# Reordering the attention stage of a two-layer graph network: key scores per feature block, two products earlier, adjacency banks later, degrees through DRAM

## The chip, the cores and the metric

The kernel runs on one core of a Trainium2 chip. The metric is the device time of one execution in microseconds (us). Three runs of the kernel before gave a median of 375.6 us. One more execution was taken with the hardware profiler; all rows quoted below are from that one.

Engines are named as in the profile: PE is TensorE's matmul side and PEld its weight loads, DVE is VectorE, ACT is ScalarE, POOL is GpSimd, SP is SyncE, which here only issues DMAs. Times inside the kernel are counted from the start of the profiled span.

## The reference, cut to what matters

The graph has N = 1250 nodes with 512 features and E = 20000 edges sorted by destination. Two layers follow each other, each behind a layer norm and a ReLU. The change touches the first one:

```python
h  = relu(layernorm(x))
xn = batchnorm(h)                                  # over the nodes
agg = segment_sum(xn[src], dst) / max(deg, 1)      # deg: edges per destination
conv = relu(agg @ W_conv + b_conv)
# attention over the first 256 nodes, 8 heads of 64, 256 random features (proj)
q, k, v = heads(h[:256] @ Wq), heads(h[:256] @ Wk), heads(h[:256] @ Wv)
phi(t) = exp(t*s @ proj.T - 0.5*sum((t*s)**2) - max) / sqrt(256) + 1e-6
kv  = phi(k).T @ v
att = (phi(q) @ kv) / (phi(q) @ phi(k).sum() + 1e-6) @ Wo
x = x + batchnorm(conv + att + h)
```

For keys the max runs over all nodes of a head, for queries over one row. The second layer (a sum over neighbours and two dense layers) is not touched.

## The kernel before, in words

**Opening (`tile_gnn`).** The edge lists are read as overlapping pieces, and for each group of 10 destinations the 256 edges that hold its own are picked by matmuls with 0/1 matrices (L1568, tile `keys`: 20 passes for the sources, 20 for the destinations). DVE then splits the keys into `js`, `prow`, `kcol` (L1606 to L1608) and ACT copies `dist` (L1609). TensorE is kept busy meanwhile by matmuls on zeros (`keep_up`, L1517: six ahead of the counting `cnt`, three ahead of `keys`). A branch on `bad` follows; the arm taken is `sorted_graph`.

**Attention stage (`sorted_graph`, L137 to L527).** Four kinds of work share the engines:

- *The adjacency matrix*, 25 banks of 50 destinations. `onehots` (L198) makes two 0/1 tiles on DVE (`op` and `ok`, L206), `count` (L213) multiplies them in ten matmuls on PE, and ACT copies the bank to `adj` (L220). The one-hot tiles have two buffers, the banks two PSUM buffers (`acc`), which `product` shares.
- *Nodes.* `layernorm_relu` (L86) takes statistics on DVE (L96), scales on ACT (L105), PE transposes (L226) and ACT copies to `hT` (L227). Nodes 0 and 1 come from the opening, eight tiles of nodes follow.
- *Keys and queries.* `features` (L236) multiplies four blocks of weights with `hT` (L245, eight passes each), scales and squares them on ACT (L249, L251), and sums the squares per head in `pd` by a matmul with the 128 x 8 tile `half` (L248, L253). `scores` (L263) multiplies with the projection into the one PSUM tile `sc`. For keys ACT copies it to `kf` (L333) and DVE takes the maximum `kmx` (L334); `kf` gets its exponentials later (L376). Values are L337.
- *`product(j)`* (L416): batch norm of tile j of the nodes (`normed`), four matmuls with `W_conv` (L422, eight passes), and the result split into `hi` and `lo`.

`beside()` is a generator that yields after each piece of this; the loop at L404 takes one bank between two of its pieces, 15 banks in all. In it, all four key blocks come first, then the eight key scores with the values, then the queries. After it the loop at L493 runs ten turns: `query(i)`, `product(i)`, in turn 1 all of `keyvalue` (L449), in turns 2 to 7 `degrees` (L428: one-hot tile, two matmuls, maximum and reciprocal on 128 x 210 elements), one bank, `turn(i-1)` (L472) and `attend(i-2)` (L482). The output projection (L521) ends the stage, and the sum over neighbours (L575) follows from 135 us on.

Each engine runs its instructions in a fixed order, which a scheduler sets when the kernel is built; `order(...)` around an instruction keeps those so marked in the order of the program.

Of the kernel before, what the change touches and what calls it, by code (L numbers as in the profile page):

```python
# [23 lines left out]
KD = D // 128  # L24
# [45 lines left out]
def sorted_graph(ctx: ExitStack, tc: tile.TileContext, ed, x, n1g, n1b, n2g, n2b, wconv, bconv,  # L70
# [99 lines left out]
    load_x(x1, (NT, NT + 1), (NT + 1, NT + 3), (NT + 3, NJ - 1))  # L170
# [17 lines left out]
    half = ap1.tile([128, KD, HEADS], F32, name="half")  # L188
    nc.gpsimd.memset(half, 0.0)
    for b in range(KD):  # L190
        for a in range(2):
            nc.gpsimd.memset(half[a * 64:a * 64 + 64, b, 2 * b + a:2 * b + a + 1], 0.5)
# [20 lines left out]
    def count(bt, op, ok):  # L213
        acc = accp.tile([S, NJ, TB], F32, name="acc", tag="acc")
        for q in range(BG):
            for i in range(2):
                nc.tensor.matmul(acc[:, :, q * TG:(q + 1) * TG], op[:, q, :, i],  # L217
                                 ok[:, q, :, i].rearrange("p (j t) -> p j t", t=TG),
                                 start=(q == 0 and i == 0), stop=(q == BG - 1 and i == 1), skip_group_check=True)
        nc.scalar.copy(adj[:, :, bt * TB:(bt + 1) * TB], acc)  # L220
# [15 lines left out]
    def features(wt, name):  # L236

        tT = ap1.tile([128, KD, TOK], F32, name=f"{name}T", tag="tT")
        dg = ap1.tile([128, NT, HEADS], F32, name=f"{name}_dg")

        pd = mm.tile([HEADS, TOK], F32, name="mm")
        for b in range(KD):
            ps = mm.tile([128, TOK], F32, name="mm")
            for k in range(KD):
                nc.tensor.matmul(ps, wt[:, k, b * 128:(b + 1) * 128], hT[:, k, :TOK],  # L245
                                 start=(k == 0), stop=(k == KD - 1))
            if b:
                nc.tensor.matmul(pd, half[:, b - 1, :], sq, start=(b == 1), stop=False)  # L248
            nc.scalar.activation(tT[:, b, :], ps, AF.Copy, scale=DH ** -0.25)  # L249
            sq = ap2.tile([128, TOK], F32, name="sq")  # L250
            nc.scalar.activation(sq, tT[:, b, :], AF.Square)  # L251
            yield
        nc.tensor.matmul(pd, half[:, KD - 1, :], sq, start=False, stop=True)  # L253
        d8 = ap2.tile([HEADS, TOK], F32, name="d8", tag="sq")
        nc.scalar.copy(d8, pd)
        yield
        ps = mm.tile([128, NT, HEADS], F32, name="mm")
        for t in range(NT):
            nc.tensor.transpose(ps[:, t, :], d8[:, t * 128:(t + 1) * 128], ident[:HEADS, :HEADS])
        nc.vector.tensor_copy(dg, ps)  # L260
        return tT, dg

    def scores(tT, t, b):  # L263

        ps = sc.tile([128, 2, 512], F32, name="sc")
        for a in range(2):
            nc.tensor.matmul(ps[:, a, :M], tT[a * 64:a * 64 + 64, b, t * 128:(t + 1) * 128],  # L267
                             projT[a * 64:a * 64 + 64, :], start=True, stop=True)
        return ps[:, :, :M]
# [11 lines left out]
    def normed(j, engine):  # L281
        n = ROWS[j]
        xn = ap2.tile([128, KD, S], F32, name="xn")
        for f in range(KD):
# [3 lines left out]
            else:  # L288
                nc.vector.tensor_scalar(xn[:, f, :n], src, gain, shift, op0=ALU.mult, op1=ALU.add)
        return xn  # L290

    def beside():

        first_nodes()
        ps = mm.tile([128, M], F32, name="mm")
        for c in range(2):
            nc.tensor.transpose(ps[:, c * 128:(c + 1) * 128], pr[:, c].rearrange("p i d -> p (i d)"), ident)
        nc.scalar.copy(projT, ps)
        yield
        more = iter(range(NT, NJ))  # L300

        def node():
            for j in more:
                nodes([j])
                break

        keys = features(ed.wk, "k")
        try:
            while True:
                next(keys)  # L310
                node()
                yield
        except StopIteration as end:
            kT, kdg = end.value
        wqt = ed.wk
        nc.sync.dma_start(wqt, wq.rearrange("(k p) n -> p k n", p=128))
        ps = mm.tile([128, rows], F32, name="mm")
        nc.tensor.transpose(ps, vec, ident[:rows, :rows])
        nc.scalar.copy(vT, ps)
        nc.scalar.mul(negT, vT, -1.0)  # L320
# [6 lines left out]
        todo_stats = iter(steps)  # L327


        for n, (t, b) in enumerate(pairs):  # L330
# [3 lines left out]
            nc.vector.tensor_reduce(kmx[:, t, o:o + 2], ps, AX.X, ALU.max)  # L334
            if b == 0:
                pv = mm.tile([128, D], F32, name="mm")
            nc.tensor.matmul(pv, hT[:, b, t * 128:(t + 1) * 128], wvt[:, b, :], start=(b == 0), stop=(b == KD - 1))  # L337
            if b == KD - 1:
                nc.scalar.copy(va[:, t, :, :DH], pv.rearrange("p (h d) -> p h d", d=DH))
            if n < 3:  # L340
                node()
            else:
                stats(2)
            yield

        km1 = ap1.tile([128, HEADS], F32, name="km1")
        nc.vector.tensor_tensor(km1, kmx[:, 0, :], kmx[:, 1, :], ALU.max)
        queries = features(wqt, "q")
        next(queries)
        stats(len(steps))  # L350
# [4 lines left out]
        gmv = ap1.tile([128, KD, 2], F32, name="gmv")  # L355
        for f in range(KD):
            nc.vector.bn_aggr(gmv[:, f, :], gst[:, f].rearrange("p i s -> p (i s)"))
        nc.scalar.activation(gc[:, 0, :], gmv[:, :, 1], AF.Sqrt, bias=epsc, scale=1.0)
# [5 lines left out]
        for t in range(NT):  # L364
            nc.vector.scalar_tensor_tensor(kb[:, t, :], kmall, -1.0, kdg[:, t, :], op0=ALU.mult, op1=ALU.subtract)
        nc.vector.reciprocal(gc[:, 0, :], gc[:, 0, :])
# [5 lines left out]
        todo = iter([(t, o) for t in range(NT) for o in range(HEADS)])  # L372

        def exponentials(n):
            for t, o in itertools.islice(todo, n):
                nc.scalar.activation(kf[:, t, o, :], kf[:, t, o, :], AF.Exp, bias=kb[:, t, o:o + 1], scale=1.0)  # L376
                if o == HEADS - 1:
                    nc.vector.tensor_scalar(kf[:, t], kf[:, t], M ** -0.5, KEPS, op0=ALU.mult, op1=ALU.add)

        try:  # L380
            while True:
                next(queries)
                exponentials(4)
                if len(xns) < 2:
                    xns[len(xns)] = normed(len(xns), nc.vector)
                yield
        except StopIteration as end:
            qT[:] = end.value
        exponentials(NT * HEADS)
# [12 lines left out]
    next(rest)  # L402
    batches = iter(range(nbt))
    for piece in itertools.count():  # L404

        if not 6 <= piece < 14 or piece % 2:
            batch(next(batches))
        if next(rest, rest) is rest:
            break
# [4 lines left out]
    lo = lop.tile([S, NJ, D], F32R, name="lo", tag="lo")  # L414

    def product(j):  # L416

        n = ROWS[j]
        xn = normed(j, nc.scalar) if j not in xns else xns[j]
        ps = accp.tile([S, D], F32, name="hw", tag="acc")  # L420
        for f in range(KD):
            nc.tensor.matmul(ps[:n], xn[:, f, :n], wct[:, f, :], start=(f == 0), stop=(f == KD - 1))  # L422
        halves(hi[:n, j, :], lo[:n, j, :], ps[:n])


    rdeg = ed.wk.rearrange("p k n -> p (k n)")[:, :N]

    def degrees(g0, n):  # L428
        shape = [128, n, TG, 2]
        oh = tmp.tile(shape, F16, name="oh", tag="row")  # L430
        nc.vector.tensor_tensor(oh, ed.iok[:, :TG, :].unsqueeze(1).to_broadcast(shape),
                                ed.dist[:, g0:g0 + n].unsqueeze(2).to_broadcast(shape), ALU.is_equal)
        ps = mm.tile([128, n * TG], F32, name="mm")
        for i in range(2):
            nc.tensor.matmul(ps, ed.ones, oh[:, :, :, i].rearrange("p g t -> p (g t)"), start=(i == 0), stop=(i == 1))
        c = slice(g0 * TG, (g0 + n) * TG)
        nc.vector.tensor_scalar(rdeg[:, c], ps, 1.0, None, op0=ALU.max)
        nc.vector.reciprocal(rdeg[:, c], rdeg[:, c])
# [3 lines left out]
    qfs, qfTs = {}, {}  # L442

# [12 lines left out]
    def query(n):  # L456
# [9 lines left out]
        nc.vector.tensor_scalar(qf, qf, M ** -0.5, KEPS, op0=ALU.mult, op1=ALU.add)  # L466

    def turn(n):
# [5 lines left out]
        nc.scalar.copy(qfTs[n], pT)  # L474

    def attend(n):
# [8 lines left out]
        nc.vector.tensor_scalar(z, pa[:, :, DH], KEPS, None, op0=ALU.add)  # L485
        nc.vector.reciprocal(z, z)
        for i in range(2):
            hd = 2 * b + i
            nc.vector.tensor_scalar(ao[:, t, hd, :], pa[:, i, :DH], z[:, i:i + 1], None, op0=ALU.mult)
# [3 lines left out]
    for i in range(len(pairs) + 2):  # L493
        if i < len(pairs):
            query(i)
        product(i)
        if i == 1:
            for q4 in range(2):
                keyvalue(0, q4)
                keyvalue(1, q4)  # L500
        if 2 <= i < 8:
            degrees(21 * (i - 2), min(21, NGR - 21 * (i - 2)))
        for bt in itertools.islice(batches, 1):
            batch(bt)
        if 1 <= i <= len(pairs):
            turn(i - 1)
        if i >= 2:
            attend(i - 2)

    aT = ap1.tile([128, KD, TOK], F32, name="aT", tag="tT")  # L510
# [473 lines left out]
def any_graph(ctx: ExitStack, tc: tile.TileContext, ed, x, src, dst, n1g, n1b, n2g, n2b, wconv, bconv,  # L984
# [8 lines left out]
    ident = const.tile([128, 128], F32)  # L993
    make_identity(nc, ident)
    ones = const.tile([128, 128], F32)
    nc.vector.memset(ones, 1.0)
    epsc = const.tile([128, 1], F32)
    nc.vector.memset(epsc, EPS)
# [440 lines left out]
def tile_gnn(ctx: ExitStack, tc: tile.TileContext, x, src, dst, *rest):  # L1439
# [11 lines left out]
    ed.dist = pre.tile([128, NGR, 2], I16, name="dist")  # L1451
# [6 lines left out]
    with tc.tile_pool(name="raw", bufs=1) as raw, tc.tile_pool(name="rawp", bufs=1, space=PSUM, side="right") as rawp:  # L1458

        kd, ks = (raw.tile([KS, SPAN], I32, name=name) for name in ("kd", "ks"))  # L1460
        kd16, ks16 = (raw.tile([KP, SPAN], F16, name=name) for name in ("kd16", "ks16"))
        few = E - (KP - 1) * STEP * RB
# [183 lines left out]
```

## Time and profile before

| what | value |
|---|---|
| median of 3 runs | 375.6 us (373.75 to 375.77) |
| the profiled execution | 375.39 us, span of its instructions 373.6 us |
| PE, DVE, ACT busy | 356.9, 235.8, 157.0 us |
| opening, up to the first one-hot tile | 0 to 12.0 us |
| attention stage | 12.0 to 135.4 us |
| sum over neighbours of the first layer | 135.4 to 183 us |
| second layer | 183 to 373.6 us |

The page gives each engine's busy time; the chain of work that ended last tells for each moment which engine the end waited for; the table by stretches gives busy time per engine in a stretch of time, with TensorE's granted clock. A matmul row shows the duration of one pass with its way through the array; passes overlap, so what a group costs PE is the distance from its start to the next group's start, and that is what the chain's rows give. An f32 matmul is two passes.

### The profile page before, as it was taken

How to read it: one execution, taken by the hardware profiler on the slowest of the kernel's cores; microseconds unless marked ns; L12 is line 12 of the kernel's file. 1: busy time of each engine (PE TensorE's matmuls, PEld its weight loads, DVE VectorE, ACT ScalarE, POOL GpSimd, SP SyncE). 2: the span in 40 equal slices, each digit the busy share in tenths (PEclk: the TensorE clock that was granted, in tenths of full speed). 3: DMA queues.
4: the chain of work that ended last, by engine and by line, in shares of the span. 5: the costliest groups of instructions: out<-in, count | busy, mean ns of one | idle time of the engine just before them, and what ended most of it. 6: DMA issues, size and time to landing. Idle time of an engine off the chain costs nothing.

```text
span 373.6 us, 4916 instructions
## 1 busy us (share of the span) xinstructions
PE 356.9 (96%) x1840; PEld 262.6 (70%) x1840; DVE 235.8 (63%) x585; ACT 157.0 (42%) x310; POOL 35.4 (9%) x55
## 2 busy tenths in 40 slices
PE   8799979999999999999999999999999999999981
PEld 4665555676565699998768888777777777777761
DVE  6899994648897325677888223172881788414673
ACT  5598549727574360111056503132552552122211
POOL 3100000000000005000000009620053000000000
PEclk9999999999999999999999999999999999999996
DMA  6853020000000372000000000050000000000124
GB/s 209 277 185 118 11 103 0 0 3 2 0 1 2 126 269 105 0 3 0 0 2 0 2 0 1 24 203 0 0 2 1 1 2 0 1 0 11 59 84 130
DMA packets 13285, 18.06 MB, mean 48 GB/s; under 512 B 1341, under 2 KB 6658, under 8 KB 13254
## 3 DMA queue, kind: packets, MB, share of 16 engines
q1 hardware_dynamic: 12542, 17.34, 13.7%
q8 instruction: 16, 0.26, 0.3%
q10 hardware_dynamic: 712, 0.33, 0.3%
q14 instruction: 15, 0.12, 0.1%
HBM read 15.11 MB, written 2.56 MB: 47 GB/s over the span
## 4 chain that ended last, share of the span: by engine, by line
PE 86%; DVE 9%; ACT 2%; DMA 1%; issue 1%; DVEq 0%
PE mm L764 31%; PE mm L707 12%; PE mm L575 12%; PE hw L422 10%; PE mm L245 3%; PE mm L449 2%; PE mm L521 2%; PE mm L482 2%; PE sc L267 2%; PE acc L217 2%; DVE op L206 1%; PE mm L226 1%; PE mm L701 1%; DVE kmx L334 1%; PE mm L472 1%; DVE ok L206 1%
## 5 line engine op out<-in xcount | busy, mean ns | idle before, releaser
L422 PE MATMUL hw<-wconv,xn 128*128 128x512 f32 (+1 forms) x80 | 37.1, 604 | 0.3 <-ACT adj L220 0.3
L779 ACT ACTIVATE kept<-mm,vT 128x313 f32<-128x313 f32 x36 | 18.5, 521 | 42.9 <-PE mm L764 41.8
L707 PE MATMUL mm<-hi,adj 128*128 128x512 f32 (+2 forms) x100 | 32.1, 399 | 0.5 <-DVE hi L655 0.4
L707 PE MATMUL mm<-lo,adj 128*128 128x512 f32 (+2 forms) x100 | 31.6, 394 | 0.0
L129 ACT ACTIVATE r<-mv,epsc 128x1 f32<-128x1 f32 x16 | 4.7, 292 | 61.6 <-DVE mv L128 61.6
L764 PE MATMUL mm<-hid,w 128*128 128x313 f32 x96 | 25.9, 427 | 0.0
L422 PEld LDWEIGHTS hw<-wconv,xn 128*128 128x128 f32 (+1 forms) x80 | 14.1, 187 | 16.4 <-issue 14.8
L575 PE MATMUL mm<-adj,lo 128*128 128x416 f32 (+3 forms) x120 | 25.1, 355 | 0.0
L575 PE MATMUL mm<-adj,hi 128*128 128x416 f32 (+3 forms) x120 | 25.1, 355 | 0.0
L206 DVE TENSOR_TENSOR op<-iop,prow 128x1280 f16<-128x1280 f16 (+2 forms) x27 | 20.7, 768 | 6.0 <-PE acc L217 5.6
L784 DVE TENSOR_TENSOR hid<-mm,kept 128x313 f32<-128x313 f32 x24 | 10.9, 478 | 20.4 <-ACT kept L779 16.9
L764 PEld LDWEIGHTS mm<-hid,w 128*128 128x128 f32 x96 | 18.1, 190 | 6.9
L575 PEld LDWEIGHTS mm<-adj,hi 128*128 128x128 f32 x120 | 21.9, 189 | 1.1
L575 PEld LDWEIGHTS mm<-adj,lo 128*128 128x128 f32 x120 | 21.8, 189 | 1.0
L707 PEld LDWEIGHTS mm<-hi,adj 128*128 128x128 f32 (+2 forms) x100 | 18.4, 186 | 5.8 <-DVE hi L655 1.4
L698 DVE SCALAR_TENSOR_TENSOR z<-h,e,mm 128x512 f32<-128x512 f32 (+1 forms) x10 | 7.0, 744 | 23.5 <-PE mm L707 15.7
L707 PEld LDWEIGHTS mm<-lo,adj 128*128 128x128 f32 (+2 forms) x100 | 18.5, 186 | 4.6 <-DVE lo L648 0.2
L217 PEld LDWEIGHTS <-op 128*128 128x128 f16 x250 | 13.7, 97 | 9.1 <-issue 4.7
L217 PE MATMUL acc<-ok,op 128*128 128x100 f16 x250 | 16.2, 207 | 3.3 <-DVE ok L206 2.7
L702 ACT COPY zT<-mm 128x512 f32<-128x512 f32 (+1 forms) x10 | 5.3, 582 | 29.3 <-PE mm L701 29.3
L764 PE MATMUL mm<-tz,w 128*128 128x313 f32 x64 | 17.5, 426 | 0.0
L764 PE MATMUL mm<-hid,sw 128*128 128x313 f32 x64 | 17.5, 427 | 0.0
(253 smaller groups left out, 704.6 us busy)
## 6 DMA issues: line engine op xcount, KB each, us to landing
w<-in_L_gnn_W_dram SPq DMA_DIRECT2D x2, 2048.0 KB
xs<-in_x_dram SPq DMA_DIRECT2D x1, 2304.0 KB
out_dram<-xs SPq DMA_DIRECT2D x7, 256.0 KB
wk<-in_L_gnn_Wk_dram SPq DMA_DIRECT2D x1, 1024.0 KB
x<-in_x_dram SPq DMA_DIRECT2D x1, 1024.0 KB
v<-in_L_gnn_Wv_dram SPq DMA_DIRECT2D x1, 1024.0 KB
wconv<-in_L_gnn_W_conv_dram SPq DMA_DIRECT2D x1, 1024.0 KB
wk<-in_L_gnn_Wq_dram SPq DMA_DIRECT2D x1, 1024.0 KB
```

The costliest lines, as they stand in the source:

```text
L206: i = nc.vector.tensor_tensor(t[:, qs], iota.unsqueeze(1).to_broadcast(shape), keys[:, bt, qs].unsqueeze(2).to_broadcast(shape), ALU.is_equal)
L217: nc.tensor.matmul(acc[:, :, q * TG:(q + 1) * TG], op[:, q, :, i], ok[:, q, :, i].rearrange("p (j t) -> p j t", t=TG), start=(q == 0 and i ...
L245: nc.tensor.matmul(ps, wt[:, k, b * 128:(b + 1) * 128], hT[:, k, :TOK], start=(k == 0), stop=(k == KD - 1))
L267: nc.tensor.matmul(ps[:, a, :M], tT[a * 64:a * 64 + 64, b, t * 128:(t + 1) * 128], projT[a * 64:a * 64 + 64, :], start=True, stop=True)
L422: nc.tensor.matmul(ps[:n], xn[:, f, :n], wct[:, f, :], start=(f == 0), stop=(f == KD - 1))
L449: nc.tensor.matmul(ps[:, i, :], kf[:, t, hd, mb * 128:(mb + 1) * 128], va[:, t, hd, :], start=(t == 0), stop=(t == NT - 1))
L482: nc.tensor.matmul(pa[:, i, :], qfTs[n][:, i, mb, :], kv[:, mb, hd, :], start=(mb == 0), stop=(mb == 1))
L575: nc.tensor.matmul(ps, part[:k, j, fs], adj[:k, j, c], start=(part is hi and j == 0), stop=(part is lo and j == NJ - 1))
L707: nc.tensor.matmul(ps[:n], adj[:k, j, t * S:t * S + n], part[:k, j, :], start=(part is hi and j == 0), stop=(part is lo and j == NJ - 1))
L764: order(nc.tensor.matmul(banks[i], left[:, k, m * 128:(m + 1) * 128], right[:, k, i * NH:(i + 1) * NH], start=(p in (1, 2, 5) and k == 0), ...
L779: nc.scalar.activation(t[:, c, :], self.A[c], AF.Identity, bias=self.part(i, 0, c)[1], scale=1.0)
L784: order(nc.vector.tensor_tensor(self.part(i, j, c)[0], self.B[c], t[:, c, :], ALU.add))
```

## The change

In the opening, the destination list is loaded in two tiles (`kd`, 160 columns, and `ahead`, the other 240), so that `sample` needs the first alone; `keys` becomes two PSUM tiles, one for each kind; `dist` is no longer copied by ACT but worked out from `js` and `kcol` on DVE; `keep_up` runs 7 and 4 matmuls instead of 6 and 3. Key scores follow right behind each block of key features, nodes are taken in pairs, the values lie between the scores. The half sums of squares become four matmuls with 32 columns each, into four quarters of one PSUM tile. Queries are scaled and squared on DVE. `product(0)` and `product(1)` stand beside the exponentials, ten banks come ahead of the loop instead of 15, and the loop takes 15. `degrees` turns the matmul around (the edges are the stationary side, a column of ones moves), takes reciprocals of a 128 x 11 tile, writes it to DRAM and reads it back to all partitions. The constant of `phi(q)` is added while the transposed tile is copied.

```diff
-    load_x(x1, (NT, NT + 1), (NT + 1, NT + 3), (NT + 3, NJ - 1))
+    load_x(x1, (NT, NT + 2), (NT + 2, NT + 4), (NT + 4, NJ - 1))
...
@@ count
+                if bt < 2:
+                    order(m)
...
@@ features
+        squares = ap2.tile([128, KD, TOK], F32, name="sq", bufs=1)
...
-            if b:
-                nc.tensor.matmul(pd, half[:, b - 1, :], sq, start=(b == 1), stop=False)
...
+            if name == "k":
+                nc.scalar.activation(tT[:, b, :], ps, AF.Copy, scale=DH ** -0.25)
+                nc.scalar.activation(sq, tT[:, b, :], AF.Square)
+            else:
+                nc.vector.tensor_scalar(tT[:, b, :], ps, DH ** -0.25, None, op0=ALU.mult)
+                nc.vector.tensor_tensor(sq, tT[:, b, :], tT[:, b, :], ALU.mult)
+            yield tT
+        pd = mm.tile([128, TOK], F32, name="mm")
+        for b in range(KD):
+            order(nc.tensor.matmul(pd[b * QUAD:(b + 1) * QUAD], half, squares[:, b, :], start=True, stop=True,
+                                   skip_group_check=True))
...
@@ beside
+        for b in range(KD):
+            kT = next(keys)
...
+            nodes([NT + 2 * b, NT + 2 * b + 1])
+            yield
+            for t in range(NT):
+                keys_scores(t, b)
+                values(1 if b else 0)
+            yield
...
+        exponentials(4)
+        next(queries)
+        for n in range(2):
+            xns[n] = normed(n, nc.vector)
+        yield
+        exponentials(4)
+        next(queries)
+        yield
+        exponentials(4)
+        product(0)
+        next(queries)
+        yield
+        exponentials(NT * HEADS)
+        product(1)
...
-    for piece in itertools.count():
-        if not 6 <= piece < 14 or piece % 2:
-            batch(next(batches))
...
+    for n in (0, 0, 1, 1, 0, 0, 1, 0, 0, 1, 1, 1):
+        some(n)
+        next(rest)
...
+    for _ in rest:
+        some(1)
+    some(1)
...
@@ degrees
+        if b0 == 0:
+            nc.vector.scalar_tensor_tensor(dist, ed.js, -float(JK), ed.kcol, op0=ALU.mult, op1=ALU.add)
...
+                nc.tensor.matmul(ps[:w, b:b + 1], oh[:, h0:h1, :, i].rearrange("p g t -> p (g t)"), ed.ones[:, :1],
+                                 start=(i == 0), stop=(i == 1), skip_group_check=True)
...
+            nc.vector.reciprocal(deg, deg)
...
+            nc.sync.dma_start(row[0, :end].rearrange("(k p) -> p k", p=full), deg[:full, :some])
+            nc.sync.dma_start(row[0, end:].rearrange("(k p) -> p k", k=1), deg[:N - end, some:])
+            nc.sync.dma_start(rdeg, row[:, :].to_broadcast([128, N]))
...
@@ query
-        nc.vector.tensor_scalar(qf, qf, M ** -0.5, KEPS, op0=ALU.mult, op1=ALU.add)
@@ turn
-        nc.scalar.copy(qfTs[n], pT)
+        nc.scalar.activation(qfTs[n], pT, AF.Identity, bias=keps, scale=1.0)
@@ the loop
-        product(i)
-        if i == 1:
-            for q4 in range(2):
-                keyvalue(0, q4)
-                keyvalue(1, q4)
-        if 2 <= i < 8:
-            degrees(21 * (i - 2), min(21, NGR - 21 * (i - 2)))
-        for bt in itertools.islice(batches, 1):
-            batch(bt)
+        if i < 2:
+            keyvalue(0, i)
+            keyvalue(1, i)
+        else:
+            product(i)
+        if 2 <= i < 5:
+            degrees(4 * (i - 2), min(4, DB - 4 * (i - 2)))
+        some(1)
...
+        if i in (1, 3, 5, 7, 8):
+            some(1)
...
@@ the opening
-        edges(nc.sync, kd, dst, 0, 112, 0, SPAN)
+        edges(nc.sync, kd, dst, 0, 112, 0, own)
...
+        edges(nc.sync, ahead, dst, 0, 112, own, SPAN, own)
...
-        keep_up(6)
+        keep_up(7)
...
-        keys = rawp.tile([128, 2, 2, NGR], F32, name="keys")
+        keys = [rawp.tile([128, 2, NGR], F32, name=f"keys{kind}") for kind in range(2)]
...
-        keep_up(3)
+        keep_up(4)
...
-        order(nc.scalar.copy(ed.dist, dist))
```

The changed instructions' order on each engine, as built, is used below: PE runs the first key block, then the transposes of node tiles 2 and 3, bank 0, both key scores of block 0, bank 1, key block 1, and so on. On DVE the maximum of the first key score stands behind the one-hot tiles of bank 2, that of the second behind three more sets of statistics.

## The prediction

> **What bounds the kernel now.** I read the page's first part, then the table by stretches, then the chain in order of time. On the page PE is busy nearly throughout:
>
> ```profile
> PE 356.9 (96%) x1840; PEld 262.6 (70%) x1840; DVE 235.8 (63%) x585; ACT 157.0 (42%) x310; POOL 35.4 (9%) x55
> ```
>
> The last changed line runs before 135.4 us, where the sum over neighbours starts; behind it the code is the same. So the question is when that point comes. The table by stretches (start:end, length, busy time of PE, PEld, DVE, ACT, POOL, clock, DMA share, GB/s):
>
> ```profile
> 38.00:53.00 15.00, 13.02 (x100) 7.45 (x100) 14.86 (x35) 8.36 (x17) 0.00 (x0) 1.00 0.21 70
> 63.00:80.00 17.00, 16.99 (x112) 12.20 (x114) 10.33 (x20) 10.60 (x27) 0.00 (x0) 1.00 0.00 1
> 80.00:127.00 47.00, 47.00 (x273) 28.45 (x272) 35.72 (x84) 26.57 (x61) 0.00 (x0) 1.00 0.01 1
> ```
>
> Up to 53 us DVE is full and PE has gaps; from 63 us PE is full and DVE has room. The chain says the same (start, us, what):
>
> ```profile
> 49.91 0.73 DVE op L206
> 50.65 0.59 DVE ok L206
> 51.24 0.74 DVE op L206
> 51.97 0.61 DVE kmx L334
> ...
> 52.72 0.70 PE sc L267 x4
> ...
> 55.35 0.53 PE mm L248 x2
> ...
> 80.50 3.63 PE hw L422 x8
> 84.13 0.19 PE mm L435 x2
> 84.31 0.46 PE acc L217 x10
> 84.77 0.45 PE mm L472 x4
> 85.22 0.84 PE mm L482 x8
> 86.07 0.63 PE sc L267 x4
> ```
>
> A key score waits for a maximum that DVE reaches only behind one-hot tiles; a turn of the loop (3.63 + 0.19 + 0.46 + 0.45 + 0.84 + 0.63 = 6.20) is PE alone. Hence the DVE work that goes from the loop (reciprocals L438 8.7 us, maxima L437 2.3, L466 3.4) is worth nothing by itself. What counts is PE work and PE's gaps.
>
> **The opening.** Its chain starts with 2.56 us of destinations; `sample` runs at 3.40. With 640 bytes a row instead of 1600 I take 3.05 (bounds: 2.63, where DVE comes free, and 3.40). The zeros cost PE 0.43 each, so seven from 1.19 end at 4.2, and counting starts there instead of 4.48. A fourth zero ahead of `keys` takes that back: 1.14 (count) + 0.24 + 0.53 (leads) + 4 x 0.43 puts it near 7.7 instead of 7.52.
>
> ```profile
> 7.52 2.04 PE L1568 MATMUL keys<-pick,ks 124*128 124x125 f16 x20
> 9.40 1.29 PE L1568 MATMUL keys<-pick,kd 124*128 124x125 f16 x20
> 10.74 0.42 DVE L1606 TENSOR_SCALAR js<-keys 128x250 f32<-128x250 f32 x1 [1.59 <-PE keys L1568]
> 11.52 0.41 DVE L1608 SCALAR_TENSOR_TENSOR kcol<-js,keys 128x250 int16<-128x250 f32 x1
> 11.99 0.42 DVE L206 TENSOR_TENSOR op<-iop,prow 128x512 f16<-128x512 f16 x1
> ```
>
> `js` waited 1.59 us for 40 passes; with two tiles it needs the first 20. Then only `kcol` waits for the rest, and the one-hots start near 11.2 instead of 11.99 (bounds: 12.2, the late zeros alone; 10.4, where all 40 passes run at the second row's pace of 57 ns and not the first's 94). ACT no longer copies `dist` ahead of the copies to `hT` (12.74), so the first key block, which stood behind bank 0 at 15.38, runs from about 12.3 to 14.0, and the projection's transposes end at 14.2.
>
> **To the first node transposes.** DVE: 11.2 + 1.47 (four one-hots, 11.99 to 13.46) + 0.41 (`dist`, priced as `kcol`) + 4 x 0.62 (statistics) + 0.6 (aggregates) + 0.3 (root's reciprocal, shift) = 16.5; ACT's scaling 0.81; PE transposes at 17.4 instead of 19.78. The nodes must have landed by 13: 0.13 MB of projection and 0.5 MB of nodes issued from about 9.3, at the 282 GB/s of 10 to 15 us, are there at about 13. If not, add what is missing. PE idles from 14.2 to 17.4: its order puts banks 0 and 1 behind these transposes.
>
> **From there to the end of the exponentials.** Before: 19.78 to 67.13, where `product(0)` ends, 47.35 us. After, to the end of `product(1)`, ten banks and the first 12 passes of L449:
>
> - Half sums: before 4 x 0.53 = 2.12 each for keys and queries. After, eight passes into four column quarters. The trace has no column quarters; the nearest row is the score, whose four passes on two row halves take 0.63 (two at a time, 0.31 a pair). Four at a time this gives 0.63; bounds 0.44 and, one after another, 2.12. I take 0.63: -2.98.
> - Banks: 112 of the 150 count passes lay in the old stretch, now all 100 of ten banks do: -1.2 x 0.46 = -0.55.
> - `product(1)` +3.49, L449 +12 x 0.11 = +1.33. One key score more (before, it was done at 17.93) and one query score less: 0.
> - Gaps that go: 0.24 and 0.20 near 40, then 0.61, 0.69, 0.95 behind the `kmx` of 49 to 53, 0.42 at 62.5: -3.1.
> - Gaps that come: `sc` has one buffer. The first key score ends at 17.4 + 0.45 + 0.35 (ACT) + 0.45 + 0.46 + 0.63 = 19.75; its `kmx` stands behind bank 1's one-hots 1.47, three statistics 1.86, small work 0.65 and bank 2's one-hots 1.32, and ends at 22.4: +2.65, and the 0.35. For the other six scores DVE keeps about level with PE (per block: two one-hot sets 2.65, two maxima 1.2, four bn_stats 2.0, against PE's 1.73 + 0.9 + 1.26 + 1.9 + 0.92 = 6.7); I add 0.7, bounds 0 and 6 x 1.32.
>
> Sum: 47.35 - 2.98 - 0.55 + 4.82 - 3.1 + 3.7 = 49.25, so this ends at 66.65. Queries scaled on DVE (8 x 0.4) lie in its gap of 53 to 63, where it was busy 4.40 of 10 us; without that cover the same 0.4 would stand ahead of each score. Wq is issued behind the last key block (about 40) and took 5 us before (28.0 to 33); its first use is near 48.
>
> **The rest.** Before, 67.13 to 135.37 = 68.24. After: -3.49 (`product(1)`) -1.33 (L449) +0.63 (query 0) + 5 x 0.46 (banks) = 66.35. Degrees: 12 passes of 0.095 become 22 short ones; at the 46 ns of a count pass that is even. Their DMAs stand on SP behind Wo and ahead of `xs`, around 95 us, and are used at about 140; 45 us cover them. The `xs` load behind them was issued at 125.8 and is read at 154. DVE gains five one-hot sets (6.6) and loses over 14. So the stage ends at 133.0 instead of 135.4: **-2.4 us, 375.4 - 2.4 = 373.0**. The profiled run's 375.39 stands 0.2 under the median; 0.5% (1.9 us), about what a measurement tells from no change, puts the border near 373.7.
>
> **A rule against it: the clock.** The trace first:
>
> ```profile
> 362.00:367.50 5.50, 2.68 (x19) 1.78 (x17) 5.10 (x17) 1.29 (x3) 0.00 (x0) 1.00 0.37 110
> 367.50:373.60 6.10, 0.00 (x0) 0.00 (x0) 0.58 (x1) 0.00 (x0) 0.00 (x0) 0.50 0.41 123
> ```
>
> PE had waited 2.51 us (before 365.75), run ten short passes, and was at half clock by 367.5. After the change it idles 3.2 us and then 2.65, which the attention stage before never does. In the opening it took 3.4 us of unbroken work (5.74 to 9.17) until passes went from 106 to 57 ns; at half pace that loses 1.7 us. The Trainium skill's "TensorE: Matmul & The Clock Gate", section "What's actually happening", halves the clock after an idle window of about 3.4 us; by that rule 3.2 us could pass free, by the row above it need not. The measured row decides: this is a rival with 1.7 us.
>
> **Rivals.**
> 1. *Forecast*, 373.0 (372.0 to 374.3): chance 0.45.
> 2. *Better*: early full pace (one-hots at 10.4, 0.8 less), no 0.7 of waits, half sums at 0.44 (0.4 less): 371.1; for it speak seven zeros without a gap; against it the landings. 0.17.
> 3. *Clock falls* in the new idle: 373.0 + 1.7 = 374.7. For it: the row at 367.5. Against it: stretches like 13 to 16 with half of PE idle kept the clock. 0.25.
> 4. *Slower*: the single score tile. If each maximum stands behind a one-hot set on DVE (1.32), as at 49.91 to 51.97, PE waits that long per score. Two such waits eat the gain, from four on it is slower by over 0.5%: with four 373.0 + 5.3 = 378.3. Against it: DVE's block sum of about 6 under PE's 6.7. 0.13.
>
> That the half sums run one after another (it doesn't do what it says) costs 3.0 and lands in rival 3's time. The range leaves out half of 2's best and most of 4: 370.0 to 377.2. Faster: 0.33 of 1, all of 2, 0.05 of 3; slower: 4.
>
> **What would show it.** `js` ahead of 10; first node transposes at 17 to 18; passes of L259 (after) starting 7 ns apart; a gap of 2 to 3 us on PE ahead of the second key score; transposes at 109 ns (not twice that) behind it; `product(1)` done near 66; a loop turn of 3.6 + 0.9 + 1.9; L632 starting near 133. Wrong it goes if PE shows a gap at each score, or if Wq or the nodes land late.

## The result, and the profile after

The changed kernel takes **379.55 us** (median of four executions, 377.73 to 381.46); the kernel before took 374.68 beside it (373.72 to 375.77). The ratio is 1.0127, with an interval of 1.0090 to 1.0163: **slower** by 1.3%, where 373.0 and "faster" were forecast. The profiled execution took 379.09 us, span 377.3.

The page's first line, with PE as busy as before, shows nothing of that:

```profile
PE 356.5 (94%) x1853; PEld 265.0 (70%) x1853; DVE 225.7 (60%) x562; ACT 154.7 (41%) x298; POOL 35.1 (9%) x47
```

The table by stretches (columns as before: stretch, length, PE, PEld, DVE, ACT, POOL, clock, DMA share, GB/s), first two of the stretches that were shown of before, then four stretches of 3.41 us, cut where the clock record begins and ends:

```profile
38.00:53.00 15.00, 14.04 (x97) 8.80 (x96) 11.74 (x29) 9.83 (x21) 0.00 (x0) 1.00 0.30 93
...
80.00:127.00 47.00, 47.00 (x293) 28.88 (x294) 26.32 (x66) 28.04 (x62) 0.00 (x0) 1.00 0.06 15
15.09:18.51 3.42, 0.96 (x7) 0.72 (x8) 3.30 (x12) 2.03 (x4) 0.12 (x1) 1.00 1.04 337
18.51:21.92 3.41, 2.57 (x18) 1.63 (x16) 3.08 (x9) 2.83 (x6) 0.12 (x1) 0.50 0.47 168
21.92:25.33 3.41, 2.71 (x16) 1.97 (x17) 3.34 (x11) 1.97 (x5) 0.12 (x1) 0.50 0.27 87
25.33:28.75 3.42, 3.42 (x11) 2.69 (x10) 2.32 (x6) 0.46 (x2) 0.00 (x0) 0.50 0.61 226
```

DVE has been relieved from 38 to 53 us (11.74 instead of 14.86), PE is fuller there, and the turns up to 127 us are PE alone as before. The new thing is above: TensorE's clock falls to half at 18.51 us, behind a stretch in which PE was busy for 0.96 of 3.42 us, and stays there for three stretches, 10.24 us, until one of them is full. The chain in order of time (start, us, what) runs through it:

```profile
19.09 0.85 PE acc L217 x10
...
19.96 0.82 DVE op L206
20.78 0.59 DVE ok L206
21.37 0.60 DVE ln_st L96
21.98 0.60 DVE kmx L318
...
22.62 1.22 PE sc L274 x4
23.84 0.95 PE acc L217 x10
24.79 3.56 PE mm L247 x8
```

A score (L274) takes 1.22 instead of the 0.63 to 0.70 shown of before, a bank 0.95 instead of 0.46, a key block (L247) 3.56 instead of 1.73. Ahead of the second score stands what was predicted: two one-hot tiles, statistics, and only then the maximum that frees the score tile.

The half sums, and the start of a turn of the loop, from the same view:

```profile
50.17 0.64 PE mm L259 x8
...
62.66 0.57 PE mm L259 x8
...
85.72 3.63 PE hw L418 x8
89.35 0.40 PE mm L477 x8
```

The half sums cost 0.64 and 0.57 us for eight passes; before they were four times 0.53. They are the one part whose gain is plain. A product in the loop costs its 3.63 as before, and the short passes of the degrees (L477) 0.40 in this turn where two long ones took 0.19, in three turns instead of six.

Two places at the end of the stage and of the kernel lose time too. The chain at the seam to the sum over neighbours:

```profile
136.94 0.27 ACT end L581
...
137.24 0.49 DVE hT L582
...
137.77 1.42 PE mm L632 x6
```

The first sum waits 1.03 us for DVE to read the last block of the output projection. (Gaps are counted here from where the next pass could have started, one pass of L578 behind the last one's start, at 136.74. The profile's own idle figures run from the end of the last row and are 0.16 smaller, 0.87 here.) As built, that block and the first sum share PSUM bank 0; in the kernel before, the first sum shares it with the second block, long read by then. And the last output DMAs on SP, first in the kernel before, then in the changed one (start, us; two issues in each row):

```profile
367.17 1.80 SPq L908 DMA_DIRECT2D out_dram<-xs  x2
```

```profile
369.86 2.42 SPq L965 DMA_DIRECT2D out_dram<-xs  x2
```

In both, one issue takes over a microsecond instead of 0.34 to 0.38. In the kernel before it is the last (1.36); in the changed kernel it is the last but one (1.54), and the last starts only 2.04 us behind its start. From the last DVE instruction to the end of the execution it is 8.34 us instead of 7.31.

### The profile page after: what moved, and what is told of

Same layout as the page of the kernel before. It is cut to its first block, busy times and chain, and to the rows that moved or that the text cites. A ratio compares the mean times of both kernels' runs of the same rounds, so it can differ in the third digit from the quotient of the medians.

```text
span 377.3 us, 4902 instructions
## 1 busy us (share of the span) xinstructions
PE 356.5 (94%) x1853; PEld 265.0 (70%) x1853; DVE 225.7 (60%) x562; ACT 154.7 (41%) x298; POOL 35.1 (9%) x47
## 4 chain that ended last, share of the span: by engine, by line
PE 86%; DVE 6%; ACT 3%; DMA 1%; issue 1%; SPq 1%; DVEq 0%
PE mm L821 31%; PE mm L764 12%; PE mm L632 12%; PE hw L418 9%; PE mm L247 4%; PE acc L217 3%; PE sc L274 2%; PE mm L505 2%; PE mm L578 2%; PE mm L538 2%; DMA x<-in_x_dram 1%; PE mm L325 1%; PE mm L758 1%; PE mm L527 1%; PE mm L602 1%; PE idle L1574 1%
## 5 line engine op out<-in xcount | busy, mean ns | idle before, releaser
L632 PE MATMUL mm<-adj,hi 128*128 128x416 f32 (+3 forms) x120 | 25.0, 354 | 0.9 <-DVE hT L582 0.9
L632 PE MATMUL mm<-adj,lo 128*128 128x416 f32 (+3 forms) x120 | 25.1, 355 | 0.0
L632 PEld LDWEIGHTS mm<-adj,hi 128*128 128x128 f32 x120 | 21.8, 189 | 2.3 <-DVE hT L582 1.3
L632 PEld LDWEIGHTS mm<-adj,lo 128*128 128x128 f32 x120 | 21.8, 189 | 1.0
L217 PEld LDWEIGHTS <-op 128*128 128x128 f16 x250 | 14.2, 102 | 7.3 <-issue 7.1
L247 PE MATMUL mm<-hT,wk 128*128 128x256 f32 x64 | 17.0, 416 | 0.9 <-ACT hT L229 0.9
L821 PE MATMUL mm<-zT,w 128*128 128x313 f32 x64 | 17.4, 427 | 0.0
```

Source lines behind the costliest of these rows:

```text
L217: m = nc.tensor.matmul(acc[:, :, q * TG:(q + 1) * TG], op[:, q, :, i], ok[:, q, :, i].rearrange("p (j t) -> p j t", t=TG), start=(q == 0 a ...
L247: order(nc.tensor.matmul(ps, wt[:, k, b * 128:(b + 1) * 128], hT[:, k, :TOK], start=(k == 0), stop=(k == KD - 1)))
L632: nc.tensor.matmul(ps, part[:k, j, fs], adj[:k, j, c], start=(part is hi and j == 0), stop=(part is lo and j == NJ - 1))
L821: order(nc.tensor.matmul(banks[i], left[:, k, m * 128:(m + 1) * 128], right[:, k, i * NH:(i + 1) * NH], start=(p in (1, 2, 5) and k == 0), ...
```

## The experiments

Theory after the result: **the clock** falls in the new idle stretches (1.7 us), and what is left is a sum of waits that the prediction did not see, above all the **shared bank** (1.03). Rivals: the **single score tile** costs more than counted; the **opening** costs instead of gaining; and, behind all, the new **order** itself is poor, so that nothing but a change of order brings the gain back. Ratios are to the kernel before as measured beside each run.

| run | what | median us | ratio (interval) |
|---|---|---|---|
| after | the whole change | 379.55 | 1.0127 (1.0090 to 1.0163) |
| e1_zeros | after + 27 zero matmuls in the idle | 377.07 | 1.0052 (1.0029 to 1.0075) |
| e4_few_zeros | after + 9 zero matmuls | 376.29 | 1.0024 (1.0001 to 1.0048) |
| e2_max_from_copy | after, maxima from ACT's copy | 378.08 | 1.0065 (1.0033 to 1.0097) |
| e3_banks | after, another list order of banks | 378.87 | 1.0108 (1.0065 to 1.0151) |
| c2_zeros_lastbank | e1 + last block in another bank | 376.06 | 1.0043 (1.0012 to 1.0074) |
| c1_zeros_bank_max | c2 + maxima from the copy | 375.10 | 0.9998 (0.9971 to 1.0025) |
| d1_keys_ahead | after, key blocks 1 to 3 earlier | 372.38 | 0.9903 (0.9879 to 0.9928) |
| d2_ahead_bank_max | d1 + last block's bank + maxima from the copy | 369.64 | 0.9839 (0.9810 to 0.9868) |
| b1_opening | before + the opening | 374.77 | 1.0003 (0.9977 to 1.0030) |
| b2_quarters | before + half sums in quarters | 373.35 | 0.9952 (0.9926 to 0.9978) |
| b3_opening_quarters | before + both | 372.31 | 0.9921 (0.9891 to 0.9950) |
| b4_degrees_dram | b3 + degrees by DRAM | 373.32 | 0.9937 (0.9913 to 0.9961) |

### The clock: e1_zeros and e4_few_zeros

```diff
+    def fill(n):
+        ps = accp.tile([S, 512], F32, name="fill", tag="acc")
+        for _ in range(n):
+            order(nc.tensor.matmul(ps, ed.zeros[:, :128], ed.zeros, start=True, stop=True))
...
                 nc.scalar.copy(projT, ps)
+                fill(15)
...
                 keys_scores(t, b)
+                if b == 0 and t == 0:
+                    fill(12)
```

> The changed kernel with matmuls on zeros laid into PE's two idle stretches: 15 behind the projection's transposes (3.2 us at full pace) and 12 between the two key scores of block 0 (2.6 us). They add no work to the result. Theory C (the granted clock falls in that idle, to half from 18.5 to 28.7 us): the clock stays up, the second key block (L247) takes 1.75 us instead of 3.56, and product(1) ends about 3 us earlier, near 66; the run is about 376. Theory S (PE waits for the one score tile, whatever the clock): the score waits stay as they are, the run stays at 378 to 379.

The zeros take 2.8 us off by the ratios (1.0127 to 1.0052), and the profiled execution keeps the full clock from 6.5 to 368.3 us. The second key block, in the order of time, first in the changed kernel, then with the zeros:

```profile
24.59 3.74 PE L247 MATMUL mm<-hT,wk 128*128 128x256 f32 x8
```

```profile
24.64 1.96 PE L253 MATMUL mm<-hT,wk 128*128 128x256 f32 x8
```

The granted clock of the single executions says the same: 0.971 to 0.980 in the four of the changed kernel, 0.983 to 0.991 in the ten with zeros, 0.983 to 0.994 in the kernel before. In the traces `product(1)` ends at 67.22 instead of 68.96, 1.74 us earlier, though this execution's opening came 0.53 later (first one-hot tile at 10.36 instead of 9.83, the clock up at 6.48 instead of 4.85); from the first one-hot tile on it is 2.27. The fall is worth 1.7 to 2.3 us, then. So the fall is shown, and it is not all: the kernel is still slower than before.

The second run asks how little is enough: `fill(5)` and `fill(4)` at the same places.

> The changed kernel with 5 zero matmuls in the first idle stretch and 4 in the second, instead of 15 and 12; both stretches stay idle for over half of their time. Reading of the traces so far (windows of 3.41 us in which TensorE has work for under about 0.4 lose the clock, those above keep it): the work in the windows rises to about 0.45 to 0.55, the clock holds, 377 us as with 27 zeros. Rival (any idle stretch of over about 2 us loses it): the clock falls as in the changed kernel, 379 us. In between, a fall in some executions: 378 us.

It is no slower than with 27 zeros. Its table by stretches, cut at its own clock record:

```profile
15.69:19.10 3.41, 2.02 (x12) 1.06 (x11) 3.04 (x12) 2.42 (x7) 0.12 (x1) 1.00 1.05 351
...
8.86:12.28 3.42, 1.44 (x15) 1.05 (x12) 2.96 (x9) 2.16 (x4) 0.58 (x7) 1.00 0.82 275
```

The stretch that lost the clock in the changed kernel now holds 2.02 us of work and keeps it. In this execution another stretch, with 1.44 us, loses it earlier, ahead of the zeros, and one stretch later, with 2.88 us of work, it is back: the changed kernel lives near the edge at other places too. The rival (any idle of over 2 us) is not tested here, since PE's waits at the two places came to 1.39 and 1.10 us by the profile's rows; the trace of e3_banks, next, has such a wait.

### The seam: e3_banks and c2_zeros_lastbank

```diff
-    banks = banks[4:] + banks[:4]
+    banks = banks[5:] + banks[4:5] + banks[:4]
```

> The changed kernel, where the sum over neighbours begins with another PSUM bank: the order of its seven first banks starts with the second. Theory B (the first sum's bank 0 is the one that the last block of the output projection used, so PE waits 1.03 us for L582 at 136.7): that wait goes, 1.0 us less. Rival: the wait is for the data that L582 writes, then nothing changes.

The 0.87 us of idle ahead of L632 is there as in the changed kernel, released by L582. The edit was void: as built, the first tile that is used gets bank 0, whatever its place in the list. It told nothing of the bank (the ratio does not differ from the whole change's), but its trace is a second one of the same instructions as the changed kernel's, and it bears on the clock:

```profile
17.59 1.36 PE L228 MATMUL mm<-ident,hn 128*128 128x128 f32 x8 [3.05 <-ACT hn L105]
```

PE idles for 3.05 us here and keeps the full clock, as the idle lies across two stretches with 1.48 and 2.25 us of work; so the rule of "any idle of over 2 us" is out. The clock falls one stretch later (1.34 us of work), for 3.41 us instead of 10.24, and from the first one-hot tile to the end of `product(1)` it is 57.17 us instead of 59.13. Where the stretches begin is thus worth 2 us to the same program.

For the bank, the other side was moved:

```diff
-        ps = mm.tile([128, TOK], F32, name="mm")
+        ps = sc.tile([128, 2, 512], F32, name="sc")[:, 0, :TOK] if b == KD - 1 else mm.tile([128, TOK], F32, name="mm")
         for f in range(KD):
             nc.tensor.matmul(ps, wot[:, f, b * 128:(b + 1) * 128], ...
```

> The changed kernel with the zero matmuls that keep the clock (e1_zeros, 377.07 us, which leaves the trace a wait of 1.03 us between the output projection and the first sum over neighbours), and the last block of the output projection written to a score tile, so that no bank that the first sum uses is read at the seam. Theory (the wait is for the shared PSUM bank): the gap of 1.03 us at 136 us is gone, about 376.0 us. Rival (the sum waits for something else that ends with the last vector instruction of the stage, hT or the pool's release): the gap stays, 377.0 us.

PE in order of time at the seam, first with the zeros alone, then with the block moved (L641 is the first sum here):

```profile
136.03 1.80 PE L641 MATMUL mm<-adj,hi 128*128 128x418 f32 x8 [0.87 <-DVE hT L591]
```

```profile
133.88 1.88 PE L641 MATMUL mm<-adj,hi 128*128 128x418 f32 x8
```

The wait is gone, so the bank was its cause. The medians of the two (1.0052 and 1.0043) can't show 1 us apart; the trace does.

### The score tile: e2_max_from_copy and c1_zeros_bank_max

```diff
-            order(nc.vector.tensor_reduce(kmx[:, t, o:o + 2], ps, AX.X, ALU.max))
+            order(nc.vector.tensor_reduce(kmx[:, t, o:o + 2], kf[:, t, o:o + 2, :], AX.X, ALU.max))
```

> The changed kernel with the keys' maximum taken from ACT's copy in SBUF instead of from the PSUM score tile, so that the tile is free once ACT has copied it. Theory S: the waits of PE behind kmx (2.1 us ahead of the second score, then 0.22, 0.78 and 0.42) shrink to some 0.6 in all, the run is 2 to 3 us faster than the changed kernel's 379. Theory C: the first idle stretch of 3.4 us (14.0 to 17.5) stays, so the clock still falls near 18.5; only what lies after it gains, under 1.5 us.

Alone it lets the second score follow the first by 1.91 us instead of 2.77 and shortens the later gaps, but the clock falls as before (0.974 to 0.978 in all seven executions). It gains 1.5 us by the medians and 2.3 by the ratios, between what the two theories expected, and its 1.0065 stays above 1. With the clock kept and the bank moved:

> As c2_zeros_lastbank, and the keys' maxima are taken from the copy in SBUF, so that the score tile comes free behind ScalarE's copy alone. Theory (one score tile, held by a late maximum, costs the gaps of 0.48, 0.78 and 0.41 us that the trace of e1_zeros shows ahead of the scores): these go, about 374.5 us, level with the kernel before. Rival (VectorE's own work sets the pace of this stretch, so the waits move to the one-hot tiles and the banks): 375.5 to 376 us.

375.1, level with the kernel before. Of the gaps of 0.48, 0.78 and 0.41 ahead of the scores, 0.40 and 0.27 are left, and from the first node transposes to the end of `product(1)` the trace shows 47.89 us instead of 48.84 in c2's. So the score tile is a real but small cost, about 1 us; the intervals of c1 and c2 overlap, so this size is the traces' and not the medians'. Rival 4's price of 5.3 is out.

### The order: d1_keys_ahead and d2_ahead_bank_max

```diff
         for b in range(KD):
-            kT = next(keys)
             if b == 0:
+                kT = next(keys)
...
                 nc.scalar.copy(projT, ps)
+                next(keys)
+                next(keys)
             nodes([NT + 2 * b, NT + 2 * b + 1])
...
                 keys_scores(t, b)
+                if b == 0 and t == 0:
+                    next(keys)
```

> The changed kernel with real work where it idles: the key blocks 1 and 2 ahead of the transposes of the first node pair, block 3 between the first two key scores; nothing else. Theory (three key blocks, 3 x 1.74 us, have gone from behind idle time, and the clock that falls in that idle costs 1.7 us): the idle stretch from 14 to 17.5 us is filled, the clock holds, and the kernel comes to 375 to 376.5 us from 379.55, more than the zeros gave (377.07), as zeros keep the clock but do no work. Rival (VectorE decides this stretch, so the key blocks only move the waits): level with the zeros, 377 us.

PE in order of time, with real work where the changed kernel idles from 13.95 to 17.50 us:

```profile
14.38 3.62 PE L247 MATMUL mm<-hT,wk 128*128 128x256 f32 x16
18.08 0.66 PE L228 MATMUL mm<-ident,hn 128*128 128x128 f32 x4
...
20.14 0.70 PE L274 MATMUL sc<-projT,kT 64*128 64x256 f32 x4
```

No stretch loses the clock until the end, and `product(1)` ends at 62.00 instead of 68.96, 6.96 us earlier (7.44 from the first one-hot tile on), which is what three key blocks (3 x 1.74) and the clock (1.7 to 2.3) make together. At 372.38 it beats both what was expected of the theory and of the rival: VectorE was not the limit. (The wait at the seam is absent here too, since the tiles before it fall on other banks.) The seam and the score tile on top:

> d1_keys_ahead with the last block of the output projection in a score tile and the maxima taken from the copy. If the causes named so far (clock and idle, shared bank, late score tile) are all, this meets the forecast for the change: d1 less 1.0 us for the bank and 0.5 to 1.5 for the tile, 372.5 to 374.5 us. If it stays at 375 us or above, a further cause is at work.

369.64, ratio 0.9839: the best of all, some 10 us under the changed kernel with the same work, and below the 372.5 to 374.5 that were expected before d1's result was known. The move of the last block can't have added to it, as d1 has no wait at the seam. The further gain over d1 (2.7 us by the medians; the intervals do not touch) comes in a kernel whose clock is kept, where the late maxima show as gaps: 0.61, 1.48 and 0.63 us in d1's trace, 0.29 at most in this one.

### Single parts on the kernel before: b1, b2, b3, b4

> The kernel before with the change's opening alone (destinations in two tiles, seven and four zeros, two key tiles); dist is still copied by ACT, all behind it as before. Theory O (the one-hots start near 9.9 instead of 12.0, and DVE bounds the next 40 us): 1.5 to 2 us faster than the kernel before. Rival (the nodes' landing at 13 to 15 us and the weights bound the start anyway): under 0.5 us.

The opening (loads in two tiles, `keys` in two, seven and four zeros) ends `product(0)` at 65.19 instead of 67.13, and still the median does not move by what can be measured. In its profile the clock falls at the end at 363.73, ahead of the last passes, instead of 367.52: of 1.94 us at the last bank (123.67 against 125.61), 0.8 is left in the span. The granted clock of the single executions goes with that (0.983 to 0.989 in the ten of this run, 0.991 or more in 19 of the 22 of the kernel before), but that the clock at the end takes the rest was not tried.

> The kernel before with the half sums in four column quarters for keys and queries, nothing else. If the eight passes take 0.6 us instead of 2.12 wherever TensorE decides: the queries' sums stand in the stretch where TensorE is full, -1.5 us; the keys' sums stand where VectorE decides up to 53 us, so 0 to -1.5: 372.4 to 373.9 us against 375.4. Rival: the wider copy and transposes behind them (128 rows instead of 8) give it back, 375 us or more.

```diff
-                nc.tensor.matmul(pd, half[:, b - 1, :], sq, start=(b == 1), stop=False)
...
+            nc.tensor.matmul(pd[b * QUAD:(b + 1) * QUAD], half, squares[:, b, :], start=True, stop=True,
+                             skip_group_check=True)
```

Half a per cent, inside the range expected: the quarters are worth about 2 us by themselves.

> The kernel before with the changed opening (alone 374.77 us, in its trace 1.9 us earlier at the end of the product but 0.8 us earlier at the end) and the half sums in quarters. If the two gains add: 371.5 to 373.5 us, better than the kernel before and than the whole change. Rival: the opening's gain is lost behind VectorE, which decides up to 53 us, and at the end: 374 us, that of the quarters alone.

Better than the kernel before by 0.8%, without any of the new order. Its interval overlaps that of the quarters alone, so it is not shown that the opening adds anything.

> The kernel before with the changed opening, the half sums in quarters (372.31 us) and the degrees by DRAM as in the change; order of the stages and banks as before. The prediction set the degrees at nothing: 22 short passes for 12, and VectorE's 11 us of reciprocals and maxima that go lie beside a full TensorE. By that 372 to 372.6 us. Rival for a gain: VectorE's time in the loop comes out of a turn, 371 us or less. Rival for a loss: the three DMAs delay the next loads or the short passes cost more than counted, 373 us or more.

The median of 373.32 would lie with the rival for a loss, but 0.9937 beside 0.9921 is no difference that can be told. From the end of `product(0)` to the last bank it is 58.57 us instead of 58.47, so the degrees are even, and the 11 us of VectorE that go are worth nothing there, as the prediction had it.

## Why the prediction was wrong, point by point

| step | predicted | measured |
|---|---|---|
| first one-hot tile | 11.2 (10.4 to 12.2) | 9.83 |
| first node transposes | 17.4 | 17.50 |
| half sums, eight passes | 0.63 | 0.64, 0.57 |
| second key score can start | 22.4 | 22.62 |
| later gaps ahead of key scores | 0.7 | 1.42 (1.67 at full clock, e1) |
| clock | holds (0.25 for a fall of 1.7) | fell, 1.7 to 2.3 |
| `product(1)` done | 66.65, ten banks | 68.96, nine banks |
| from there to the sum | 66.35 | 68.81 |
| sum over neighbours starts | 133.0 | 137.77 |
| from there to the end | 240.0 | 241.3 |

**Right:** the half sums to 0.06 us; the second score to 0.2 us, with the mechanism (the maximum behind the one-hot tiles of bank 2); the degrees; that DVE's relief in the loop brings nothing. The first node transposes were hit to 0.1 us by luck, as the opening came by another way than written: all 40 `keys` passes ran at full pace, since the clock was up at 4.85 instead of 9.12, so the one-hots came 1.4 us earlier than predicted; but then DVE waited 1.43 us for the nodes to land, the case that the prediction had left as "add what is missing". The two cancel. When the clock comes up differs from execution to execution (4.03 us in d1's trace, 10.05 in b2's).

```profile
L1630 PE MATMUL keys<-pick,ks 124*128 124x125 f16 x20 | 1.3, 218 | 0.0
...
L1667 DVE TENSOR_SCALAR js<-keys 128x250 f32<-128x250 f32 x1 | 0.4, 410 | 0.0
```

(Groups in the first 13 us of the changed kernel; behind the bar the busy time in us, the mean of one in ns, and the idle time before them. 20 passes for the sources in 1.3 us where 2.04 were shown of before, and `js` without the wait of 1.59 us.)

**Wrong, first step: "The clock".** The prediction had the row that loses it (the idle near 365 us) and a row that keeps it (13 to 16 us), wrote that "the measured row decides", and gave the fall 0.25. What it did not do was to put the two rows on one scale. In stretches of 3.41 us, as the clock record of the kernel before cuts them (columns as in the other tables by stretches):

```profile
12.54:15.95 3.41, 2.13 (x21) 1.78 (x22) 3.41 (x9) 1.93 (x4) 0.00 (x0) 1.00 0.96 325
364.11:367.52 3.41, 1.44 (x10) 1.04 (x10) 3.17 (x13) 1.29 (x3) 0.00 (x0) 1.00 0.49 147
```

the one that keeps the clock holds 2.13 us of PE work and the one that loses it 1.44; by the prediction's own terms for the changed kernel (PE idle from 14.2 to 17.4) a stretch laid over that idle holds only 0.2 us in the worst case, and the one that was measured held 0.96. The price was about right, 1.7 to 2.3 for 1.7, though not its length: it fell for three stretches. That waits, at half pace, kept the first two from being full enough is read from the table (2.57, 2.71, then 3.42 us of work).

**Wrong, second step: "The rest".** 66.35 was 68.81, 2.46 more. One bank is only moved there (0.46), which the gaps had pushed out of the part before. The wait at the seam (1.03, or 0.87 from the end of the last row, as the chain counts) was in no row of the kernel before, since it is a matter of which tile lies in which bank. And one query score is split: PE in order of time near 104 us,

```profile
104.37 0.70 PE L274 MATMUL sc<-projT,qT 64*128 64x256 f32 x2
105.00 0.64 PE L217 MATMUL acc<-ok,op 128*128 128x100 f16 x10
105.57 0.70 PE L274 MATMUL sc<-projT,qT 64*128 64x256 f32 x2
```

Its two halves, which elsewhere start 7 ns apart and take 0.63 together, have a bank between them and take 0.63 each: 0.62 more. These three make 2.11, or 1.95 by the chain's count; the remaining 0.35 to 0.5 was not taken apart, and rows differ by 0.1 to 0.2 there (banks, short passes).

**Third, not in the prediction: the end.** 1.30, of which 1.03 lies behind the last DVE instruction (the slow DMA issue). Behind the last DVE instruction the profiles of the kernel before and of its parts show 7.31 to 8.26 us, those of the changed kernel and its variants, which end in the same code, 7.80 to 9.32; so how much of the 1.03 comes with the change stays open. The other 0.27 is the seam again. In the kernel before, the sum's first pass starts inside the output projection's last one; in the changed kernel it can't:

```profile
135.02 2.25 PE L575 MATMUL mm<-adj,hi 128*128 128x418 f32 x10
```

```profile
137.77 2.19 PE L632 MATMUL mm<-adj,hi 128*128 128x418 f32 x10 [0.87 <-DVE hT L582]
```

The chain counts the sum from 135.37 in the first, where the projection's last pass ends, and so its first 100 passes take 19.07 us there and 19.34 in the changed kernel.

The sum in the profiles, with e1's trace for the step of the clock: 373.0 + 1.74 (clock) + 0.57 (at `product(1)`, clock taken out) + 2.46 + 1.30 = 379.07, against 379.09. The clock is shown by e1 and e4, the bank by c2; the split score and the slow issue are read from traces and were not tried alone, and what the 0.57 is made of stays open.

**The rivals.** Rival 3 (clock) happened, with its price, but in company, so that its 374.7 was 4.4 us short of the profiled execution. Rival 4 (one score tile) was at work at about a fifth of its price, and at half of it in d2's order. None of the four had the form of what decided, a sum of small losses: clock, seam, split score, end.

**What lay behind them** is in d1. The prediction worked out "PE idles from 14.2 to 17.4" and 2.65 us ahead of the second score, and booked both as the order's cost without asking what they would hold. They were enough for three key blocks whose data was there. The kernel before has all four key blocks ahead of the scores, and so has work for PE while DVE takes statistics; the change moves scores behind each block and gives that cover up. The same change with the blocks ahead has a ratio of 0.9903 (0.9879 to 0.9928) where it had 1.0127 (1.0090 to 1.0163).

The Trainium skill's "TensorE: Matmul & The Clock Gate", section "What's actually happening", gives half rate after at least one idle window of about 3.4 us and full rate after a busy one. The length agrees: the short clock records inside the traces last 3.41, 6.83, 10.24, 13.65 or 17.07 us, multiples of one length. "Idle" read as without work does not: the window that lost the clock held 0.96 us of work. The measurement decides.

## What to carry to other kernels

When an order is changed, list the idle stretches it leaves on the bounding engine and, for each, the work whose data is already there: filling two of them was worth 7 us here, more than all the parts of the change. A fixed price per part is not enough: write out how much work every stretch of the clock's length holds, and which PSUM bank or tile the next stage shares with the last reader of this one. Where zeros hold a clock, nine did as well as 27, and real work did far better.

## What the runs showed of the hardware

**The clock by stretches.** Cutting each trace at its own clock record (PE busy, in 3.41 us): the clock was lost behind stretches with 0.90 (e2), 0.96 (after), 1.34 (e3), 1.44 (e4) and 1.52 us (c1), kept behind 1.42 (b4), 1.46 (b3), 1.48 (e3), 2.00 and 2.13 (before), 2.02 (e4) and 2.48 us (e1). At half rate it stayed there behind 2.57 and 2.71 (after), 2.73 and 2.85 (e2), and came back behind 2.83 (d1), 2.88 (e4) and 3.41 (after, c1, e2, e3). So the edge lies near 1.5 us of work for losing it and near 2.85 for getting it back, and at both the two groups overlap by up to 0.1 us, so that the busy time alone decides nothing there. Where the stretches begin differs from execution to execution, which is why the changed kernel's profile lost it for 10.24 us and e3's, with the same instructions, for 3.41.

**A DMA issue beside an instruction load.** The page of the changed kernel counts packets of 16 KB under

```profile
q8 instruction: 16, 0.26, 0.3%
```

One of them starts 0.3 to 0.4 us behind PE's last pass in ten of the fourteen profiles (1.3 to 1.8 us long). Where SP's output DMA was issued 0.11 to 0.15 us ahead of it (before, e1, c2, b3), the issue took 0.34 to 0.35 us and the next one was slow; where the lead was 0.07 to 0.10 (after, e2, e3, c1, d1, b4), that issue itself took 1.54 to 2.30 and the last one started 2.0 to 2.8 us behind it instead of 0.4 to 0.9. That the packet causes it is inferred from this order, and was not tried.

**Passes on column quarters.** In the changed kernel four f32 passes of 128 x 32 start 7 ns apart and the next four 0.22 us later. In b2 only three of the quarters go together so; the fourth is a pass of its own behind them (28.14 to 28.16, then 28.38 us).
